# An attention kernel's inner rhythm: products with v in halves of 256 queries, three pairs of scores and three halves in every phase

## The chip, the cores and the metric

The kernel runs on one core of a Trainium2 chip. The metric is the device time of one execution in microseconds. A core has engines that run side by side, each through its own queue in order: TensorE (PE, matmuls; PEld is its loading of weights), VectorE (DVE), ScalarE (ACT), GpSimd (POOL) and SyncE (SP, used here to issue DMAs). They wait for each other by semaphores. TensorE writes its results to PSUM, which has eight banks of 512 float32 columns over 128 partitions.

## The reference, cut to what matters

The input x is (4, 128, 64, 64), float32: four images of 128 channels and 4096 positions. Two layers follow each other. The first is self-attention with 4 heads of 32 channels, on x normalized in 8 groups of channels:

```python
x_norm = _group_norm(x, norm_w, norm_b)
qkv = einsum('oc,bchw->bohw', qkv_w, x_norm) + qkv_b
q, k, v = split(qkv, 3, axis=1)
attn = softmax(einsum('bhid,bhjd->bhij', q, k) * 32 ** -0.5)
out = einsum('bhij,bhjd->bhid', attn, v)
x = x + einsum('oc,bchw->bohw', proj_w, out) + proj_b
```

The second is two 3x3 convolutions with weights quantized to 3 bits, each followed by batch normalization over the whole batch, with relu after the first, and relu of the sum with the layer's input after the second.

## The kernel before, in words

Attention is done in 32 blocks: four images by eight chunks of 512 queries (`blocks`; n is the block's number, b the image, qb the chunk). A block goes through 32 steps of 128 keys (`NK = 32`, kt is the step in the block). A step is:

- two *pairs* of scores (`scores`, line 425), one for heads 0 and 1, one for heads 2 and 3. q and k are held as a high and a low part in a rounded format (float32r), stacked so that two heads use the two halves of 64 rows of the array side by side. A pair is four matmuls of 512 columns, into one PSUM tile s of two banks. Its exponential (line 427, ScalarE, 128 x 1024) writes to the step's tile p in SBUF, which holds all four heads.
- the *products with v* (`weights`, line 438): for each head a float32 product of 128 keys x 32 channels by 512 queries, four heads on four column tiles of the array side by side, accumulated over all 32 steps in one PSUM bank, acc. A float32 product shows in the trace as two matmuls and two weight loads, so a step has eight.
- the addition of p to the running sum of the softmax's denominator (line 450, VectorE, 128 x 2048), or in six steps of a block (`MOVED`) a DMA that adds p to a second sum rm (line 445).

PSUM is full: the pool pss has three tiles s (six banks), psa has two banks, one of which is the block's acc. The other serves all small products, one after another. The pool ppool has eight tiles p; two of them hold the first image's x until its last projection is done, in block 1.

The order on the engines is written by hand (`manual_schedule`). Scores run ahead of products: `run_scores(2)`, and then `for s, w in ((3, 1), (3, 2)): run_scores(s); run_weights(w)`, that is three pairs, one step's products, three pairs, two steps' products, and so on. A run of scores and the run of products after it is called a phase here. Scores and products use the array in different tilings, so each phase changes tiling twice.

Beside this a block has side work, listed by `schedule(n, before)` as (step, function) and called after that step's products:

- for the block before: the sums over keys (l, line 467), their way through DRAM to be inverted and spread (`spread`, `invert`, `gather`), `weigh` (line 514), `project` (po, line 301), and the residual and store;
- for the next image: statistics (gm, gv, gb, lines 249 to 280) and the projections to q, k and v of a chunk of 512 positions (pq, pk, pv, line 301), in two halves each and an evacuation, which for q and k is ScalarE for the high part (line 335) and then VectorE for the low part (line 336), for v VectorE alone (line 355). They are written to DRAM and loaded again as needed. For the first image most of this is in a prelude and in blocks 0 and 1;
- in blocks 25 to 30 the quantization of the convolutions' weights on VectorE (`pieces`).

Small products use the column tiling of the products with v. They are put at `slots`, the steps with (32 n + kt) mod 3 = 0, so at the end of the phases with one step's products. `visit` puts the two halves at one slot or at two, and the evacuation one step later.

After attention come the convolutions (line 722).

Of the kernel before, what the change touches and what calls it, by code (L numbers as in the profile page):

```python
# [25 lines left out]
D = 32  # L26
TAPS = 9
FB = 512
# [50 lines left out]
def _fast_body(ctx, tc, x, norm_w, norm_b, qkv_wt, qkv_b, proj_wt, proj_b,  # L79
               w1, alpha1, gamma1, beta1, w2, alpha2, gamma2, beta2, out, cnt):  # L80
    nc = tc.nc
# [4 lines left out]
    NB = N // FB  # L86
    NK = N // P
    KB = FB // P
# [127 lines left out]
    sums = att.enter_context(tc.tile_pool(name="sums", bufs=2))  # L216
# [5 lines left out]
    def f32(t):  # L222
        return t.bitcast(F32)
# [204 lines left out]

    def weights(step):
        n, kt = divmod(step, NK)
        v = vs[blocks[n][0], kt // KB]
        pt = pts[step]
        if kt == 0:
            acc[n] = psa.tile([P, FB], F32, name=f"acc{n}", tag="a")
        for h in range(HEADS):
            nc.tensor.matmul(acc[n][h * D : (h + 1) * D, :], v[:, kt % KB, h * D : (h + 1) * D],  # L438
                             pt[:, h, :], start=(kt == 0), stop=(kt == NK - 1))
        if kt in MOVED:  # L440
            if kt == MOVED[0]:
                msum[n] = rpool.tile([P, HEADS, FB], F32, name=f"rm{n}", tag="rm")
                nc.gpsimd.dma_start(out=msum[n], in_=pt)  # L443
            else:
                nc.gpsimd.dma_start(out=msum[n], in_=pt, accum_op=ALU.add)  # L445
        elif kt == 1:
            rsum[n] = sums.tile([P, HEADS, FB], F32, name=f"r{n}", tag="r")
            nc.vector.tensor_tensor(rsum[n], pts[step - 1], pt, ALU.add)  # L448
        elif kt > 1:
            nc.vector.tensor_tensor(rsum[n], rsum[n], pt, ALU.add)  # L450
# [123 lines left out]
    def first_chunk(j, what, start):  # L574
        return project_parts(0, j, lambda: halves[j // 4][:, j % 4, :], start)[what]
# [2 lines left out]
        load_k(b, j)  # L578
        load_v(b, j)

    for what, j in (("k", 0), ("q", 0), ("k", 1), ("v", 0), ("k", 2), ("v", 1), ("k", 3), ("v", 2)):
        for f in first_chunk(j, what, True):
            f()
        if what == "v":
            load_k(0, j + 1)


# [1 line left out]
    late, xin = {}, {}  # L589
# [4 lines left out]
    def schedule(n, before):  # L594
        b, qb = blocks[n]
        todo = []
        slots = [kt for kt in range(NK - 1) if (n * NK + kt) % 3 == 0]
        two = b + 1 < B and qb in (2, 3)
        full = two or n == 1

        def add(kt, f):
            todo.append((kt, f))

        def visit(kts, first, second, evacuate=None):
            add(kts[0], first)
            add(kts[-1], second)
            if evacuate:
                add(kts[-1] + 1, evacuate)

        if before:  # L610
            add(1, before["merge"])
            kts = slots[3:4] if full else slots[3:5]
            visit(kts, lambda: before["sums"](0), lambda: before["sums"](1))
            kt = kts[-1]
            add(kt + 1, before["spread"])
            add(kt + 3, before["invert"])
            add(kt + 4, before["gather"])
            add(kt + 6, before["residual"])
            add(slots[9] - 2, before["weigh"])
            add(slots[9], before["project"])  # L620
            add(slots[9] + 1, before["store"])
        if n + 1 < len(blocks):
            add(14, lambda: load_q(*blocks[n + 1]))
        if n == 0:
            for kt, what, j in ((0, "k", 4), (2, "q", 1), (3, "v", 3), (6, "k", 5), (9, "k", 6),
                                (12, "v", 4), (15, "k", 7), (18, "v", 5), (21, "v", 6),
                                (24, "v", 7)):
                visit((kt,), *first_chunk(j, what, False))
                if what == "k":
                    add(kt + 2, lambda j=j: load_k(0, j))  # L630
        if n == 1:
            for i, j in zip((0, 1, 2, 4, 5, 6), range(2, NB)):
                visit(slots[i : i + 1], *first_chunk(j, "q", False))
        if b + 1 < B:
            if qb == 1:
                st = small.tile([P, NB, 6], F32, name=f"st{b + 1}", tag="st")
                for j in range(NB):
                    add(3 * j // 2, lambda j=j: fetch(b + 1, j))
                    add(3 * j // 2 + 3, lambda j=j: nc.vector.bn_stats(st[:, j, :], xin[b + 1, j]))
                late[b] = norm_parts(b + 1, st)  # L640
                add(15, late[b][0])
                for i in (0, 1):
                    add(slots[7 + i], late[b][1 + 2 * i])
                    add(slots[7 + i] + 1, late[b][2 + 2 * i])
            if qb == 2:
                add(slots[0], late[b][5])
                add(slots[0] + 1, late[b][6])
            chunks = {1: (), 2: (0, 1), 3: (2, 3), 4: (4,), 5: (5,), 6: (6,), 7: (7,)}
            for i, j in enumerate(chunks.get(qb, ())):
                p = project_parts(b + 1, j, lambda j=j: xin[b + 1, j])  # L650
                if not two:
                    places = dict(k=slots[0:2], q=slots[5:7], v=slots[7:9])
                elif i == 0:
                    places = dict(k=slots[1:2], q=slots[2:3], v=slots[4:5])
                else:
                    places = dict(k=slots[5:6], q=slots[6:7], v=slots[7:9])
                    add(8, lambda j=j: fetch(b + 1, j))
                for what, kts in places.items():
                    visit(kts, *p[what])
            if qb > 0 and qb + 1 in chunks:  # L660
                add(22, lambda j=chunks[qb + 1][0]: fetch(b + 1, j))
            if qb == NB - 1:
                for j in range(NB - 1):
                    add(4 * j + 1, lambda j=j: load_kv(b + 1, j))
        if b > 0 and qb == 0:
            add(1, lambda: load_kv(b, NB - 1))
        if b == B - 1 and 0 < qb < NB - 1:
            for kt in range(1, NK - 1, 5):
                add(kt, lambda: next(pieces, None))
        if n == len(blocks) - 1:  # L670
            add(5, lambda: load_band(0, 0))
            add(13, lambda: split_band(0, 0))
            add(17, lambda: load_band(0, 1))
            add(24, lambda: split_band(0, 1))
        return sorted(todo, key=lambda t: t[0])

    pieces = (piece for task in quant_tasks(stage) for piece in task())
    steps = len(blocks) * NK
    at = {"pair": 0, "step": 0}
    todo, parts = [], {}  # L680

    def side(kt):
        while todo and todo[0][0] <= kt:
            todo.pop(0)[1]()

    def run_scores(count):
        for _ in range(min(count, 2 * steps - at["pair"])):
            scores(at["pair"])
            at["pair"] += 1

    def run_weights(count):
        for _ in range(min(count, steps - at["step"])):
            n, kt = divmod(at["step"], NK)
            if kt == 0:
                assert not todo
                todo[:] = schedule(n, parts.get(n - 1))
            weights(at["step"])
            at["step"] += 1
            if kt == NK - 2:
                parts[n] = finish_parts(n)  # L700
            if kt == NK - 1:
                parts[n]["copy"]()
            else:
                side(kt)

    run_scores(2)
    while at["step"] < steps:
        for s, w in ((3, 1), (3, 2)):
            run_scores(s)
            run_weights(w)  # L710

# [592 lines left out]
```

## Time and profile before

| | |
|---|---|
| time | 2590.79 us, median of 3 runs (2589.92 to 2592.28) |
| span of the profiled run | 2588.2 us |
| attention, from the first to the last product with v | 34.4 to 2265.8 us |
| PE busy | 2517.2 us (97%) |
| DVE busy | 2140.3 us (83%) |
| ACT busy | 2081.9 us (80%) |
| s, line 425, 8192 matmuls | 1162.3 us busy |
| acc, line 438, 8192 matmuls | 1021.1 us busy |
| chain that ended last | PE 88%, DVE 5%, issue 3%, DMA 2%, ACT 1% |

A row of the profile's groups gives the line of the code, the engine and operation, what it writes and reads with shapes, the count, then busy time and mean duration in ns, and after the second bar the engine's idle time just before these instructions and what ended most of it. "64*128" or "128*32" on a matmul is the part of the array that it uses, rows by columns. The timeline gives start, length, engine, line and a count for a run of equal instructions, with the idle time before it and what ended it in brackets. Matmuls are pipelined: their ends are modelled, and the starts tell more. A row of busy times by stretch gives the stretch, its length and then the busy time (and count) of PE, PEld, DVE, ACT and POOL, the granted clock of TensorE, the share of DMA and GB/s.

### The profile page before, as it was taken

Reading aid. Unit: us, or ns where it says so; the run is one execution under the profiler, and the core shown is the slowest. Engines: PE = TensorE matmul, PEld = TensorE weight load, DVE = VectorE, ACT = ScalarE, POOL = GpSimd, SP = SyncE. Lnnn points to the kernel's source line nnn. Section 1 sums busy time; section 2 is a strip of 40 time slices with the busy share of each in tenths; the row PEclk is TensorE's granted clock in tenths of the full one; section 3 lists DMA queues with packets and bytes.
Section 4 is the critical chain, followed back from the end, with each engine's and each line's share of the span. In section 5 each row is a group of like instructions: output and inputs, shape, how many; then the busy total and the mean of one; then the engine's idle time right before and its main releaser. Section 6 shows DMA issues by size and latency. Waiting matters only on the chain.

```text
span 2588.2 us, 48399 instructions
## 1 busy us (share of the span) xinstructions
PE 2517.2 (97%) x20394; PEld 1223.4 (47%) x20394; DVE 2140.3 (83%) x1402; ACT 2081.9 (80%) x2275; POOL 281.4 (11%) x456
## 2 busy tenths in 40 slices
PE   6999999999999999999999999999999999999894
PEld 3444444444444444444444444444444444477773
DVE  5898888888988898888988988888999998953344
ACT  4888899999988999999988899999889898911223
POOL 2111111111011111110011111110000000100000
PEclk9999999999999999999999999999999999999997
DMA  5876766698667767697667666986655757634004
GB/s 160 191 187 172 177 161 149 154 206 201 162 148 178 178 155 171 149 225 171 160 171 161 164 159 150 207 202 142 151 130 126 154 126 148 146 80 145 1 1 164
DMA packets 147417, 400.04 MB, mean 155 GB/s; under 512 B 59240, under 2 KB 60008, under 8 KB 118648
## 3 DMA queue, kind: packets, MB, share of 16 engines
q0 software_dynamic: 45888, 280.59, 47.9%
q1 hardware_dynamic: 100728, 115.23, 16.8%
q8 instruction: 162, 2.65, 0.4%
q10 hardware_dynamic: 576, 1.05, 0.1%
q14 instruction: 63, 0.52, 0.1%
HBM read 105.32 MB, written 55.83 MB: 62 GB/s over the span
## 4 chain that ended last, share of the span: by engine, by line
PE 88%; DVE 5%; issue 3%; DMA 2%; ACT 1%; POOL 0%; SPq 0%; DVEq 0%; POOLq 0%; ACTq 0%
PE s L425 39%; PE acc L438 34%; PE c L722 9%; DVE r L450 3%; DMA rm<-p 2%; PE l L467 1%; PE po L301 1%; PE pk L301 1%; PE pq L301 1%; PE pv L301 1%; ACT p L427 1%; DVE res L844 1%; DMA xh<-in_x_dram 0%; DMA q<-qst 0%; DVE st L570 0%
## 5 line engine op out<-in xcount | busy, mean ns | idle before, releaser
L427 ACT ACTIVATE p<-s 128x1024 f32<-128x1024 f32 x2048 | 1940.2, 1034 | 235.0 <-PE s L425 158.7
L450 DVE TENSOR_TENSOR r<-r,p 128x2048 f32<-128x2048 f32 x768 | 1758.4, 2290 | 97.3 <-ACT p L427 48.1
L425 PE MATMUL s<-q,k 64*128 64x512 f32 x8192 | 1162.3, 413 | 3.9 <-ACT p L427 2.2
L438 PE MATMUL acc<-p,v 128*32 128x512 f32 x8192 | 1021.1, 601 | 0.6 <-DVE v L355 0.6
L425 PEld LDWEIGHTS s<-q,k 64*128 64x128 f32 x8192 | 711.7, 185 | 631.9 <-issue 298.0
L438 PEld LDWEIGHTS acc<-p,v 128*32 128x32 f32 x8192 | 198.6, 109 | 453.7 <-issue 446.3
L445 POOL DMA_DIRECT2D rm<-p x160 | 138.6, 866 | 950.7 <-ACT p L427 783.6
L775 ACT COPY cv<-c 128x512 f32<-128x512 f32 x64 | 37.6, 587 | 220.8 <-DVE st L774 220.8
L722 PE MATMUL c<-hi,wq 128*128 128x512 f32 x576 | 150.1, 405 | 8.3 <-DVE hi L805 6.8
L722 PE MATMUL c<-lo,wq 128*128 128x512 f32 x576 | 148.1, 402 | 0.0
L774 DVE BATCH_NORM_STATS2 st<-c 128x6 f32<-128x512 f32 x64 | 44.7, 699 | 124.5 <-PE c L722 102.5
L722 PEld LDWEIGHTS c<-hi,wq 128*128 128x128 f32 x576 | 109.4, 191 | 40.1 <-issue 8.9
L722 PEld LDWEIGHTS c<-lo,wq 128*128 128x128 f32 x576 | 109.0, 189 | 28.9
L448 DVE TENSOR_TENSOR r<-p,p 128x2048 f32<-128x2048 f32 x32 | 73.3, 2291 | 25.0 <-ACT p L427 25.0
L336 DVE SCALAR_TENSOR_TENSOR kst<-pk,b,kst 128x512 fp32r<-128x512 f32 x32 | 24.0, 751 | 73.2 <-ACT kst L335 73.2
L336 DVE SCALAR_TENSOR_TENSOR qst<-pq,b,qst 128x512 fp32r<-128x512 f32 x32 | 24.0, 750 | 41.6 <-ACT qst L335 41.6
L471 POOL DMA_DIRECT2D r<-rm x31 | 26.3, 848 | 159.8 <-PE s L425 91.9
L340 POOL DMA_DIRECT2D qd<-qst x31 | 23.3, 753 | 177.6 <-DVE qst L336 130.2
L443 POOL DMA_DIRECT2D rm<-p x32 | 17.8, 556 | 223.3 <-ACT p L427 136.4
L335 ACT ACTIVATE kst<-pk,b 128x512 fp32r<-128x512 f32 x32 | 22.4, 701 | 21.7 <-PE pk L301 21.7
L340 POOL DMA_DIRECT2D kd<-kst x28 | 20.6, 734 | 167.6 <-DVE kst L336 159.6
L467 PE MATMUL l<-r,ones 128*32 128x256 f32 (+1 forms) x504 | 37.9, 383 | 0.5 <-issue 0.5
(129 smaller groups left out, 672.0 us busy)
## 6 DMA issues: line engine op xcount, KB each, us to landing
rm<-p POOLq DMA_DIRECT2D x192, 1024.0 KB, 7.9
q<-qd SPq DMA_DIRECT2D x248, 128.0 KB
r<-rm POOLq DMA_DIRECT2D x31, 1024.0 KB, 7.1
x<-in_x_dram SPq DMA_DIRECT2D x80, 256.0 KB
k<-kd SPq DMA_DIRECT2D x124, 128.0 KB
qd<-qst POOLq DMA_DIRECT2D x31, 512.0 KB, 6.9
kd<-kst POOLq DMA_DIRECT2D x28, 512.0 KB, 4.0
y<-x POOLq DMA_DIRECT2D x32, 256.0 KB, 5.0
```

The lines of the kernel that those rows point to most:

```text
L301: nc.tensor.matmul(out[cs, :], w[:, cs], x, start=True, stop=True)
L336: nc.vector.scalar_tensor_tensor(lo, ps[what], bias, t[:, 0, :], ALU.add, ALU.subtract)
L340: (nc.sync if start else nc.gpsimd).dma_start(out=dst[b, j].rearrange("s p n -> p s n"), in_=t)
L425: nc.tensor.matmul(s[:, i, :], k[r, half, c0 : c0 + P], q[r, half, part, :], start=(part == 0), stop=(part == 1))
L427: nc.scalar.activation(pts[step][:, 2 * half : 2 * half + 2, :], s, AF.Exp, scale=SCALE)
L438: nc.tensor.matmul(acc[n][h * D : (h + 1) * D, :], v[:, kt % KB, h * D : (h + 1) * D], pt[:, h, :], start=(kt == 0), stop=(kt == NK - 1))
L445: nc.gpsimd.dma_start(out=msum[n], in_=pt, accum_op=ALU.add)
L448: nc.vector.tensor_tensor(rsum[n], pts[step - 1], pt, ALU.add)
L450: nc.vector.tensor_tensor(rsum[n], rsum[n], pt, ALU.add)
L467: nc.tensor.matmul(t["l"][h * D : (h + 1) * D, cs], ones, r[:, h, cs], start=first, stop=end)
L722: nc.tensor.matmul(ps[:, j, :].rearrange("p (r w) -> p r w", w=W), w[:, tap, :], part[:, j * RB + kh : j * RB + kh + RB, kw : kw + W], sta ...
L774: nc.vector.bn_stats(st[:, b * NB + c, :], ps[:, j, :])
```

## The change

The products with v of a step are made in two halves of 256 queries, so that the work can be cut at half steps. Every phase is now three pairs of scores and three halves, where it was three pairs and one step or two. `weights(step, half)` computes 256 columns of acc for all heads; the first half of step 0 carries the start flag for the bank, the second half of the last step the stop flag. The sum of the denominators and the moving DMAs stay once in a step, after its second half. Six pairs of scores, where it was five, run ahead of the first product.

The side work is placed by halves: p counts halves in a block (0 to 63), `ends` are the last halves of phases, which is every third, and the products may stand at any of them (where before they stood at the end of every second phase). `visit(i, ...)` puts the halves of a small product at `ends[i]` and `ends[i + 1]`, or both at `ends[i]` with `split=False`, and the evacuation at the half after. The places in blocks 0 and 1 are laid out anew: the projection of v for chunk 3 moves to the prelude, that of q for block 1 from step 2 of block 0 to its step 19, and the load of that q from step 14 to step 24.

```diff
-    def weights(step):
+    def weights(step, half):
...
-        if kt == 0:
+        if kt == 0 and half == 0:
             acc[n] = psa.tile([P, FB], F32, name=f"acc{n}", tag="a")
+        cs = slice(half * FB // 2, (half + 1) * FB // 2)
         for h in range(HEADS):
-            nc.tensor.matmul(acc[n][h * D : (h + 1) * D, :], v[:, kt % KB, h * D : (h + 1) * D],
-                             pt[:, h, :], start=(kt == 0), stop=(kt == NK - 1))
+            nc.tensor.matmul(acc[n][h * D : (h + 1) * D, cs], v[:, kt % KB, h * D : (h + 1) * D],
+                             pt[:, h, cs], start=(kt == 0 and half == 0),
+                             stop=(kt == NK - 1 and half == 1))
+        if half == 0:
+            return
...
-    for what, j in (("k", 0), ("q", 0), ("k", 1), ("v", 0), ("k", 2), ("v", 1), ("k", 3), ("v", 2)):
+    for what, j in (("k", 0), ("q", 0), ("k", 1), ("v", 0), ("k", 2), ("v", 1), ("k", 3), ("v", 2),
+                    ("v", 3)):
...
-        slots = [kt for kt in range(NK - 1) if (n * NK + kt) % 3 == 0]
+        ends = [p for p in range(2 * NK - 2) if (2 * n * NK + p) % 3 == 2]
...
-            kts = slots[3:4] if full else slots[3:5]
-            visit(kts, lambda: before["sums"](0), lambda: before["sums"](1))
...
-            add(slots[9] - 2, before["weigh"])
-            add(slots[9], before["project"])
-            add(slots[9] + 1, before["store"])
+            e = visit(5 if two else 6, lambda: before["sums"](0), lambda: before["sums"](1),
+                      split=not two)
...
+            at_half(ends[18] - 4, before["weigh"])
+            at_half(ends[18], before["project"])
+            at_half(ends[18] + 2, before["store"])
         if n + 1 < len(blocks):
-            add(14, lambda: load_q(*blocks[n + 1]))
+            add(24 if n == 0 else 14, lambda: load_q(*blocks[n + 1]))
         if n == 0:
-            for kt, what, j in ((0, "k", 4), (2, "q", 1), (3, "v", 3), (6, "k", 5), (9, "k", 6),
-                                (12, "v", 4), (15, "k", 7), (18, "v", 5), (21, "v", 6),
-                                (24, "v", 7)):
-                visit((kt,), *first_chunk(j, what, False))
+            for i, what, j in ((0, "k", 4), (2, "k", 5), (4, "v", 4), (6, "k", 6), (8, "v", 5),
+                               (10, "k", 7), (12, "q", 1), (14, "v", 6), (16, "v", 7)):
+                visit(i, *first_chunk(j, what, False), split=False)
...
         if n == 1:
-            for i, j in zip((0, 1, 2, 4, 5, 6), range(2, NB)):
-                visit(slots[i : i + 1], *first_chunk(j, "q", False))
+            for i, j in zip((0, 2, 8, 10, 12, 14), range(2, NB)):
+                visit(i, *first_chunk(j, "q", False), split=False)
...
-                    add(slots[7 + i], late[b][1 + 2 * i])
-                    add(slots[7 + i] + 1, late[b][2 + 2 * i])
+                    at_half(ends[13 + 2 * i] + (n > 1), late[b][1 + 2 * i])
+                    at_half(ends[13 + 2 * i] + 3, late[b][2 + 2 * i])
...
-    run_scores(2)
-    while at["step"] < steps:
-        for s, w in ((3, 1), (3, 2)):
-            run_scores(s)
-            run_weights(w)
+    run_scores(3)
+    while at["half"] < 2 * steps:
+        run_scores(3)
+        run_weights(3)
```

More of the change, by code (lines that the diff above doesn't have):

```diff
@@ L579, in load_kv @@
         load_v(b, j)
-    for what, j in (("k", 0), ("q", 0), ("k", 1), ("v", 0), ("k", 2), ("v", 1), ("k", 3), ("v", 2)):
+    for what, j in (("k", 0), ("q", 0), ("k", 1), ("v", 0), ("k", 2), ("v", 1), ("k", 3), ("v", 2),
+                    ("v", 3)):
         for f in first_chunk(j, what, True):
             f()
-        if what == "v":
+        if what == "v" and j < 3:
             load_k(0, j + 1)
@@ L596, in schedule, with at_half @@
         todo = []
-        slots = [kt for kt in range(NK - 1) if (n * NK + kt) % 3 == 0]
+        ends = [p for p in range(2 * NK - 2) if (2 * n * NK + p) % 3 == 2]
         two = b + 1 < B and qb in (2, 3)
-        full = two or n == 1
+        def at_half(p, f):
+            todo.append((p, f))
         def add(kt, f):
[L602 to L606, printed above, removed]
+            todo.append((2 * kt + 1, f))
@@ L607, in visit @@
+        def visit(i, first, second, evacuate=None, split=True):
+            at_half(ends[i], first)
+            e = ends[i + 1 if split else i]
+            at_half(e, second)
             if evacuate:
-                add(kts[-1] + 1, evacuate)
+                at_half(e + 1, evacuate)
+            return e
         if before:
             add(1, before["merge"])
-            kts = slots[3:4] if full else slots[3:5]
-            visit(kts, lambda: before["sums"](0), lambda: before["sums"](1))
@@ L614, in schedule @@
[L614 to L618, printed above, removed]
-            add(slots[9] - 2, before["weigh"])
-            add(slots[9], before["project"])
-            add(slots[9] + 1, before["store"])
+            e = visit(5 if two else 6, lambda: before["sums"](0), lambda: before["sums"](1),
+                      split=not two)
+            at_half(e + 2, before["spread"])
@@ L622, in schedule @@
+            at_half(e + 6, before["invert"])
+            at_half(e + 8, before["gather"])
+            at_half(e + 12, before["residual"])
+            at_half(ends[18] - 4, before["weigh"])
+            at_half(ends[18], before["project"])
+            at_half(ends[18] + 2, before["store"])
         if n + 1 < len(blocks):
-            add(14, lambda: load_q(*blocks[n + 1]))
+            add(24 if n == 0 else 14, lambda: load_q(*blocks[n + 1]))
         if n == 0:
-            for kt, what, j in ((0, "k", 4), (2, "q", 1), (3, "v", 3), (6, "k", 5), (9, "k", 6),
-                                (12, "v", 4), (15, "k", 7), (18, "v", 5), (21, "v", 6),
-                                (24, "v", 7)):
-                visit((kt,), *first_chunk(j, what, False))
+            for i, what, j in ((0, "k", 4), (2, "k", 5), (4, "v", 4), (6, "k", 6), (8, "v", 5),
+                               (10, "k", 7), (12, "q", 1), (14, "v", 6), (16, "v", 7)):
+                visit(i, *first_chunk(j, what, False), split=False)
@@ L629, in schedule @@
                 if what == "k":
-                    add(kt + 2, lambda j=j: load_k(0, j))
+                    at_half(ends[i] + 5, lambda j=j: load_k(0, j))
         if n == 1:
-            for i, j in zip((0, 1, 2, 4, 5, 6), range(2, NB)):
-                visit(slots[i : i + 1], *first_chunk(j, "q", False))
+            for i, j in zip((0, 2, 8, 10, 12, 14), range(2, NB)):
+                visit(i, *first_chunk(j, "q", False), split=False)
         if b + 1 < B:
@@ L642, in schedule @@
                 for i in (0, 1):
-                    add(slots[7 + i], late[b][1 + 2 * i])
-                    add(slots[7 + i] + 1, late[b][2 + 2 * i])
+                    at_half(ends[13 + 2 * i] + (n > 1), late[b][1 + 2 * i])
+                    at_half(ends[13 + 2 * i] + 3, late[b][2 + 2 * i])
             if qb == 2:
-                add(slots[0], late[b][5])
-                add(slots[0] + 1, late[b][6])
+                at_half(ends[0], late[b][5])
+                at_half(ends[0] + 1, late[b][6])
             chunks = {1: (), 2: (0, 1), 3: (2, 3), 4: (4,), 5: (5,), 6: (6,), 7: (7,)}
@@ L651, in schedule @@
                 if not two:
[L652 to L656, printed above, removed]
+                    for what, i in dict(k=1, q=10, v=13).items():
+                        visit(i, *p[what])
+                    continue
+                for what, i in (dict(k=2, q=7, v=9) if i == 0 else dict(k=11, q=13, v=15)).items():
+                    visit(i, *p[what], split=False)
+                if j in (1, 3):
                     add(8, lambda j=j: fetch(b + 1, j))
-                for what, kts in places.items():
-                    visit(kts, *p[what])
             if qb > 0 and qb + 1 in chunks:
@@ L678, in _fast_body, with side @@
     steps = len(blocks) * NK
-    at = {"pair": 0, "step": 0}
+    at = {"pair": 0, "half": 0}
     todo, parts = [], {}
-    def side(kt):
-        while todo and todo[0][0] <= kt:
+    def side(p):
+        while todo and todo[0][0] <= p:
             todo.pop(0)[1]()
@@ L691, in run_weights @@
     def run_weights(count):
-        for _ in range(min(count, steps - at["step"])):
-            n, kt = divmod(at["step"], NK)
-            if kt == 0:
+        for _ in range(min(count, 2 * steps - at["half"])):
+            n, p = divmod(at["half"], 2 * NK)
+            if p == 0:
                 assert not todo
                 todo[:] = schedule(n, parts.get(n - 1))
-            weights(at["step"])
-            at["step"] += 1
-            if kt == NK - 2:
+            weights(*divmod(at["half"], 2))
+            at["half"] += 1
+            if p == 2 * NK - 3:
                 parts[n] = finish_parts(n)
-            if kt == NK - 1:
+            if p == 2 * NK - 1:
                 parts[n]["copy"]()
             else:
-                side(kt)
-    run_scores(2)
-    while at["step"] < steps:
-        for s, w in ((3, 1), (3, 2)):
-            run_scores(s)
-            run_weights(w)
+                side(p)
+    run_scores(3)
+    while at["half"] < 2 * steps:
+        run_scores(3)
+        run_weights(3)
     bandlist = [(b, g) for b in range(B) for g in range(H // BR)]
```

## The prediction

> **What bounds the kernel now.** I read the page first (busy shares, then the chain), then busy times by stretch, then TensorE's timeline where no side product runs.
>
> ```profile
> PE 2517.2 (97%) x20394; PEld 1223.4 (47%) x20394; DVE 2140.3 (83%) x1402; ACT 2081.9 (80%) x2275; POOL 281.4 (11%) x456
> ...
> L427 ACT ACTIVATE p<-s 128x1024 f32<-128x1024 f32 x2048 | 1940.2, 1034 | 235.0 <-PE s L425 158.7
> L450 DVE TENSOR_TENSOR r<-r,p 128x2048 f32<-128x2048 f32 x768 | 1758.4, 2290 | 97.3 <-ACT p L427 48.1
> L425 PE MATMUL s<-q,k 64*128 64x512 f32 x8192 | 1162.3, 413 | 3.9 <-ACT p L427 2.2
> L438 PE MATMUL acc<-p,v 128*32 128x512 f32 x8192 | 1021.1, 601 | 0.6 <-DVE v L355 0.6
> L438 PEld LDWEIGHTS acc<-p,v 128*32 128x32 f32 x8192 | 198.6, 109 | 453.7 <-issue 446.3
> ```
>
> TensorE is busy 97% and is 88% of the chain. By the groups it hardly ever idles (3.9 and 0.6 us before its two great lines), but ends of matmuls are modelled, so waits under a pipelined matmul's modelled tail don't show as idle. They show in the timeline. This is TensorE alone in block 31:
>
> ```profile
> 2203.93 1.83 PE L425 MATMUL s<-q,k 64*128 64x512 f32 x12
> 2205.69 1.92 PE L438 MATMUL acc<-p,v 128*32 128x512 f32 x16
> 2207.55 1.66 PE L425 MATMUL s<-q,k 64*128 64x512 f32 x12
> 2209.14 1.06 PE L438 MATMUL acc<-p,v 128*32 128x512 f32 x8
> 2210.14 1.83 PE L425 MATMUL s<-q,k 64*128 64x512 f32 x12
> ```
>
> One score phase is always 12 matmuls, three pairs. After two steps of products with v (x16) it takes 1.66 us, after one step (x8) 1.83. The timeline of all engines at such a phase says why: the weight load for the third pair waits for an exponential.
>
> ```profile
> 1206.33 0.76 PEld L425 LDWEIGHTS s<-q,k 64*128 64x128 f32 x8 [0.84 <-ACT p L427]
> 1206.33 1.83 PE L425 MATMUL s<-q,k 64*128 64x512 f32 x12
> 1207.43 0.30 PEld L425 LDWEIGHTS s<-q,k 64*128 64x128 f32 x4 [0.34 <-ACT p L427]
> ```
>
> There are three score banks (pool pss), so pair n+3 needs the exponential of pair n. From raw starts: score matmuls follow each other every 232 ns, but the third pair starts 292 ns after its predecessor and its second half 337 later: 60 ns of waiting and 105 of restart, 0.165 us, the difference of 1.83 and 1.66. A score phase with a side product before it doesn't wait (block 10):
>
> ```profile
> 753.82 1.07 PE L438 MATMUL acc<-p,v 128*32 128x512 f32 x8
> 754.70 1.05 PE L301 MATMUL pk<-x,wn 128*32 128x256 f32 x16
> 755.68 1.67 PE L425 MATMUL s<-q,k 64*128 64x512 f32 x12
> ```
>
> So the waits sit in cycles without side products. Added up from start-to-start gaps over the trace, everything above 232 ns inside score phases is 27.4 us: 16.7 in blocks 0 to 24 and 10.7 in blocks 25 to 31. The page agrees: 8192/12 = 682.7 phases x 1.66 = 1133, against 1162.3 busy, 29 over.
>
> One stretch has another limit. Busy by stretch, blocks 24, then 25 to 28 (weights quantized on VectorE), then the last three:
>
> ```profile
> 1721.40:1788.50 67.10, 67.10 (x538) 28.53 (x540) 59.08 (x31) 60.48 (x66) 6.20 (x8) 1.00 0.70 158
> 1788.50:2066.50 278.00, 273.25 (x2156) 116.37 (x2148) 263.51 (x207) 244.96 (x267) 25.01 (x32) 0.99 0.63 140
> 2066.50:2265.80 199.30, 199.30 (x1586) 84.59 (x1584) 182.80 (x104) 179.44 (x194) 18.99 (x29) 1.00 0.64 138
> ```
>
> The fields are length, then PE, PEld, DVE. VectorE is at 95% in the middle one and PE idles 4.75 us, all before the projection: the list of waits has PE po behind DVE av (the product of line 514), 4.8 us in 3 waits.
>
> **The skill.** "TensorE: Matmul & The Clock Gate", section Back-to-back issue gap, gives columns over clock plus a fixed 2.5 ns per matmul. The trace agrees: groups of four products on four column tiles start every 429 to 430 ns at 512 columns and every 216 at 256 (l, pk, pq), that is 426.7 + 2.7 and 213.3 + 2.7. "TensorEngine Tiling (Array Packing)", Key Properties, says that changing tiling mode drains the engine. The trace agrees: last product to first score is 542 ns where 429 is normal, first score to second 340 where 232 is, and the first product follows 326 after the last score, with 454 to the second: some 0.34 us for each pair of switches. "PSUM — Partial Sum Buffer", The four PSUM rules, says that a first-matmul flag clears a whole bank and that a later one without it overwrites where bits are clear; so half 1 may go without a start, and costs no clearing.
>
> **The change, part by part.**
>
> *Phases of 3 and 3 for 3,1 and 3,2.* Per three steps there are still six pairs, three steps and four switches, so no drain is saved or added. From a score phase's start to the next, without a wait: 2210.14 - 2207.55 = 2.59 us with one step; half a step is 0.43; so 3.02. The exponentials: the first starts 0.78 after the score phase's start, they follow every 0.91, and the third ends 3.64 after it (read at 1203.74: ends at 1207.38). Now the third pair is wanted 1.04 after a phase start: in the short phase at 2.59 + 1.04 = 3.63, too early by what is seen; in an even phase at 3.02 + 1.04 = 4.06, with 0.37 to spare beyond a hop of 0.05. ScalarE needs 3 x 0.91 = 2.74 of 3.02. The waits go: -27.4.
>
> *VectorE's stretch.* In blocks 26 and 28 a faster PE only meets VectorE at the projection, as it does now. I leave them their share (2.1 + 1.5): +3.6.
>
> *Halves.* Each step has four pass groups of 256 for two of 512: 4 x 216.0 - 2 x 429.3 = 5.4 ns, x 1024 = +5.5 us. Twice as many weight loads of 109 ns lie beside passes of 216; pk, l and pq of the same shape run with no gap, and pv of 128 columns at 109 ns, so neither loading nor issue binds. Of a phase's three halves the latest need is the first exponential of the same phase, for the third half: ready 0.78 + 1.03 = 1.8 after the phase start, wanted at 1.27 (last score) + 0.33 + 0.24 + 3 x 0.216 = 2.5. No wait.
>
> *Side products at all ends.* Same matmuls, in the same tiling mode as the products with v, at ends of phases as before: no cost by themselves. A bank of psa still has two phases between most products. Their evacuations on ScalarE (0.70 us for k and q, 0.59 for copies, some 0.1 of it overlapped) stand between exponentials: with one, the third exponential ends 0.3 later than 3.64, just inside 4.06 - 0.05. I allow +2 for those that don't fit (127 such evacuations, a wait of 0.1 to 0.2 in one of eight or so). Queued behind are the exponentials, and PE for them.
>
> *Block 0.* Now q for block 1 follows k4 by two steps and v3 follows q by one, and both wait for VectorE's evacuation of the one free bank (1.52 and 2.38 us in brackets), after which the clock halves for a phase:
>
> ```profile
> 41.29 1.07 PE L301 MATMUL pq<-xh,wn 128*32 128x256 f32 x16 [1.52 <-DVE kst L336]
> ...
> 47.33 1.25 PE L301 MATMUL pv<-wn,xh 128*32 128x128 f32 x32 [2.38 <-DVE qst L336]
> 48.50 2.93 PE L425 MATMUL s<-q,k 64*128 64x512 f32 x12
> ```
>
> With v3 in the prelude (0.87 us of PE, beside the wait for q's first load) and three steps between others these go: -1.5 - 2.4 - (2.93 - 1.66) = -5.2. Starting with six pairs for five delays the first product by one exponential and a restart, less than 1.2: +1.2. The q product of block 1 comes at step 19 with its load at step 24, needed by about step 29. Eight issues at some 0.5 to 0.75 us and a landing of about 5 (q's first copies took 4.7) against 5 steps x 2.1: bound 0 to 3, I take +1.
>
> *Block 1.* The product q7 is put at the end where gm is only then read out; PE may wait behind VectorE's additions (2.29 each): 0 to 3, I take +1. Fetch and load moves otherwise lie beside PE.
>
> Sum: -27.4 + 3.6 + 5.5 + 2 - 5.2 + 1.2 + 1 + 1 = -18.3; 2590.8 - 18.3 = 2572.5 us.
>
> **Rivals.** (a) *ScalarE's waits only move.* Evacuations use up the 0.37 us, and VectorE, at 88% in the steady blocks, meets evacuations half a step earlier and waits for ScalarE (now 73 us over 32 of kst, 2.3 each) with additions queued behind; p tiles then come free late. Half of the 27.4 stays: 2586. For it: ScalarE is 90% busy in block 24. Against: blocks 4 to 7 with these evacuations have only 0.3 to 0.4 us of excess now. (b) *VectorE's stretch gains as well*, because its waits at the projection shrink with the even rhythm, and the allowances (4 us) aren't needed: -18.3 - 3.6 - 4 = 2565. Against: line 450 and the quantization are untouched. (c) *Slower.* New waits of a microsecond per block: scores now run one more pair ahead in every other phase, so a p tile lives 0.5 us longer, while adding DMAs hold it 7.9 us (one of 14 is in the chain at 160); with two of eight tiles holding x in blocks 0 and 1 this bites first. 32 x 1 - 18.3 = +14: 2604. Against: now all exponentials wait for such DMAs only 4.1 us in 5 waits. If each of the 2048 added pass groups exposed its load of 109 ns it would be +223, which the 216 ns of l rules out.
>
> **Numbers.** Forecast 0.6, (a) 0.16, (b) 0.12, (c) 0.12. Range 2560 to 2588: the low end is (b) with the waits at the projection gone too (-4.8), the high end (a) and a little more; (c) is left out. A time under 2585.6 is faster, over 2596 slower: forecast, (b) and over half of (a), which lies at that edge, make 0.81 faster; the rest of (a) and the edge of (c) 0.08 the same; the rest of (c) 0.11 slower.
>
> **What would show it.** Right: score phases of 12 at 1.66 throughout and no 1.83; L425 busy near 1135; products x24 of 256 columns at 216; phase to phase 3.03; no bracketed waits before pq and pv in block 0. Wrong: a score phase over 1.75 in blocks 3 to 24; 256-column groups slower than 220; PE idle before q, l or gm in blocks 0 and 1; VectorE or ScalarE above 95% in steady blocks.

## The result: 2605.7 us for 2590.9, slower by 0.57%

| | before | after |
|---|---|---|
| time, median | 2590.85 us | 2605.72 us |
| ratio, 95% interval | | 1.0057 (1.0039 to 1.0074) |
| span of the profiled run | 2588.2 us | 2604.2 us |

The forecast was 2572.5 us and faster; the time lies above its range and on the other side. It is close to the 2604 of the rival (c); how far (c) was right is said below. These lines of the page of after answer to those shown of before; lines 427 and 425 are as they were, line 450 is now 454, line 438 is now 439.

```profile
PE 2510.7 (96%) x28586; PEld 1491.3 (57%) x28586; DVE 2139.2 (82%) x1402; ACT 2086.3 (80%) x2275; POOL 281.6 (11%) x456
...
PE s L425 35%; PE acc L439 31%; PE c L729 9%; DMA rm<-p 6%; DVE r L454 5%; PE po L301 1%; PE l L471 1%; PE pk L301 1%; PE pq L301 1%; ACT p L427 1%; PE pv L301 1%; DVE res L851 1%; DMA tk<-in_L_conv_w_dram 0%; DMA xh<-in_x_dram 0%; DVE qst L336 0%
...
L427 ACT ACTIVATE p<-s 128x1024 f32<-128x1024 f32 x2048 | 1950.3, 1032 | 245.7 <-PE s L425 181.1
L425 PE MATMUL s<-q,k 64*128 64x512 f32 x8192 | 1146.0, 411 | 15.8 <-ACT p L427 14.5
L439 PE MATMUL acc<-p,v 128*32 128x256 f32 x16384 | 1029.2, 384 | 1.0 <-DVE v L355 1.0
```

PE's busy time fell by 6.5 us while the span grew by 16. The scores are busy for 16 us less and now have 14.5 us of real idle time in front of them, ended by exponentials, and the DMAs that add p to rm make 6% of the chain, where they made 2%. So the short waits went and others came. TensorE's timeline in block 24 has both:

```profile
1738.55 1.50 PE L439 MATMUL acc<-p,v 128*32 128x256 f32 x24
1739.98 1.66 PE L425 MATMUL s<-q,k 64*128 64x512 f32 x12
1741.58 1.50 PE L439 MATMUL acc<-p,v 128*32 128x256 f32 x24
1743.01 1.19 PE L425 MATMUL s<-q,k 64*128 64x512 f32 x8
1745.06 0.73 PE L425 MATMUL s<-q,k 64*128 64x512 f32 x4 [0.85 <-ACT p L427]
```

A phase is x12 at 1.66 us and x24, 3.03 us from score to score: as forecast. Then one score phase breaks in two. The timeline of ScalarE at that place says what it waited for:

```profile
1743.98 3.77 ACT L427 ACTIVATE p<-s 128x1024 f32<-128x1024 f32 x4 [1.29 <-DMA rm<-p]
```

The exponential had no free p tile, since a moving DMA was still reading the oldest one. ScalarE's waits for such DMAs (us in total, times, longest), before and then after:

```profile
ACT p L427 <- DMA rm<-p: 4.1, 5, 2.1
...
ACT p L427 <- DMA rm<-p: 23.6, 17, 2.9
```

The lengths of the stretches (us, cut at the first product with v of a block), with and without the moving DMAs (experiment 2):

| blocks | before | after | before, no moving DMAs | after, no moving DMAs |
|---|---|---|---|---|
| 0 | 79.4 | 72.8 | 79.5 | 72.8 |
| 1 | 76.2 | 81.6 | 74.3 | 82.4 |
| 2 to 24 | 1598.5 | 1615.0 | 1597.7 | 1594.5 |
| 25 to 28 | 278.0 | 279.6 | 274.6 | 273.2 |
| 29 to 31 | 199.3 | 197.4 | 199.6 | 197.1 |

Block 0 gained, block 1 lost, and blocks 2 to 24 lost 16 where they should have gained.

### The profile page after: what moved, and what is told of

The parts are those of the page before. It is cut to its first block, busy times and chain, and to the rows that moved or that the text cites. A ratio compares the mean times of both kernels' runs of the same rounds, so it can differ in the third digit from the quotient of the medians.

```text
span 2604.2 us, 64736 instructions
## 1 busy us (share of the span) xinstructions
PE 2510.7 (96%) x28586; PEld 1491.3 (57%) x28586; DVE 2139.2 (82%) x1402; ACT 2086.3 (80%) x2275; POOL 281.6 (11%) x456
## 4 chain that ended last, share of the span: by engine, by line
PE 80%; DVE 8%; DMA 7%; issue 4%; ACT 1%; POOL 0%; SPq 0%; DVEq 0%; POOLq 0%; ACTq 0%
PE s L425 35%; PE acc L439 31%; PE c L729 9%; DMA rm<-p 6%; DVE r L454 5%; PE po L301 1%; PE l L471 1%; PE pk L301 1%; PE pq L301 1%; ACT p L427 1%; PE pv L301 1%; DVE res L851 1%; DMA tk<-in_L_conv_w_dram 0%; DMA xh<-in_x_dram 0%; DVE qst L336 0%
## 5 line engine op out<-in xcount | busy, mean ns | idle before, releaser
L425 PE MATMUL s<-q,k 64*128 64x512 f32 x8192 | 1146.0, 411 | 15.8 <-ACT p L427 14.5
L439 PE MATMUL acc<-p,v 128*32 128x256 f32 x16384 | 1029.2, 384 | 1.0 <-DVE v L355 1.0
L439 PEld LDWEIGHTS acc<-p,v 128*32 128x32 f32 x16384 | 462.9, 109 | 486.9 <-issue 250.8
L449 POOL DMA_DIRECT2D rm<-p x160 | 139.1, 870 | 866.2 <-ACT p L427 625.4
L301 PE MATMUL po<-av,wp 128*32 128x512 f32 x256 | 35.2, 624 | 9.1 <-DVE av L518 9.1
```

The lines of the kernel that those rows point to most:

```text
L301: nc.tensor.matmul(out[cs, :], w[:, cs], x, start=True, stop=True)
L425: nc.tensor.matmul(s[:, i, :], k[r, half, c0 : c0 + P], q[r, half, part, :], start=(part == 0), stop=(part == 1))
L439: nc.tensor.matmul(acc[n][h * D : (h + 1) * D, cs], v[:, kt % KB, h * D : (h + 1) * D], pt[:, h, cs], start=(kt == 0 and half == 0), stop= ...
```

## The experiments

Each run's ratio is to the kernel before, run beside it on the same chip, and the interval behind it is the 95% one. "After" is the changed kernel. It was timed in four executions (2601.8 to 2609.4 us), and its own interval is 4.5 us to either side, so a gain that is given against it is uncertain by some 5 us.

**1. Halves alone.** In the kernel before:

```diff
-        for h in range(HEADS):
-            nc.tensor.matmul(acc[n][h * D : (h + 1) * D, :], ...
+        for half in range(2):
+            cs = slice(half * FB // 2, (half + 1) * FB // 2)
+            for h in range(HEADS):
+                nc.tensor.matmul(acc[n][h * D : (h + 1) * D, cs], ...
```

> The kernel before, with its own rhythm and places of side work, only each step's products made in two halves of 256 queries one after the other. Theory that halves cost what the pass groups say: 1024 steps x 5.4 ns, +5.5 us, 2596. Rival, that the halves themselves (twice the weight loads) cost what was lost and what was hoped for: +20 us or more, 2611.

2593.9 us, ratio 1.0007 (0.9999 to 1.0016). The busy time of the products is

```profile
L440 PE MATMUL acc<-p,v 128*32 128x256 f32 x16384 | 1026.6, 383 | 0.6 <-DVE v L355 0.6
```

that is 5.5 us over the 1021.1 of before. The halves cost what their pass groups say, or less, and aren't the loss.

**2. No moving DMAs, in both kernels.**

```diff
         if kt in MOVED:
-            if kt == MOVED[0]:
-                msum[n] = rpool.tile(...)
-                nc.gpsimd.dma_start(out=msum[n], in_=pt)
-            else:
-                nc.gpsimd.dma_start(out=msum[n], in_=pt, accum_op=ALU.add)
+            pass
```

> The kernel before without the DMAs that add p to rm, and without the merge: six of 32 steps are left out of the denominators. Every theory: ScalarE waits for these DMAs 4.1 us now, so 2586 to 2590; it is the base for the run beside it.

> The changed kernel without the DMAs that add p to rm, and without the merge: six of 32 steps are left out of the denominators. Theory that p tiles held by late moving DMAs are what the even rhythm ran into: the long waits of score phases in blocks 3 to 24 go, and the time falls by 20 us or more, to 2585 or below; what is left over the forecast are the waits in blocks 1, 2, 10, 26 and 28. Rival, that places of side products and their evacuations cost it: the long waits stay and it is above 2600.

Before: 2583.8 us, ratio 0.9971 (0.9960 to 0.9981), 7 us less, a little more than was expected. After: 2578.0 us, ratio 0.9946 (0.9930 to 0.9963), 28 us less. So the moving DMAs and what they do to other transfers cost the changed kernel some 20 us more than the kernel before, and the changed kernel without them is the faster of the two. Its timeline of TensorE at the same place in the program, block 24:

```profile
1730.02 1.63 PE L425 MATMUL s<-q,k 64*128 64x512 f32 x12
1731.58 1.50 PE L439 MATMUL acc<-p,v 128*32 128x256 f32 x24
1733.01 1.65 PE L425 MATMUL s<-q,k 64*128 64x512 f32 x12
1734.60 1.50 PE L439 MATMUL acc<-p,v 128*32 128x256 f32 x24
```

In each block from 2 to 31 all score phases together exceed their 1.66 us by less than 0.2 us, but for block 28, where one phase takes 2.93 us after its wait for the projection. So evacuations on ScalarE, for which the forecast kept 2 us, don't reach TensorE. These are the scores without moving DMAs, before and then after:

```profile
L425 PE MATMUL s<-q,k 64*128 64x512 f32 x8192 | 1159.6, 412 | 2.0 <-DMA q<-qst 1.6
...
L425 PE MATMUL s<-q,k 64*128 64x512 f32 x8192 | 1141.1, 410 | 2.5 <-DMA q<-qst 1.9
```

But without moving DMAs the change is worth only 5.9 us (2583.8 to 2578.0), a third of the 18.3 that were forecast. By the table block 0 gives 6.7 us, blocks 2 to 24 give 3.2 and blocks 25 to 31 give 3.9, and block 1 takes 8.1 back.

**What makes them late.** Worked out from the instructions and landings in the traces, mean over all blocks, in us: how long after its step's last exponential a moving DMA goes out, and how long after that it lands.

| step | 4 | 9 | 14 | 19 | 24 | 28 |
|---|---|---|---|---|---|---|
| before: goes out | 3.1 | 1.3 | 0.8 | 1.1 | 1.2 | 2.5 |
| before: lands | 5.2 | 7.7 | 8.8 | 9.4 | 8.7 | 7.8 |
| after: goes out | 5.7 | 1.7 | 1.3 | 2.6 | 4.3 | 5.0 |
| after: lands | 5.4 | 7.9 | 8.9 | 11.3 | 8.3 | 8.1 |

A tile's exponential and the one that takes the tile again lie 15.3 to 15.8 us apart before and 15.0 to 16.3 after, by step, so the time to reuse has hardly changed; the DMA takes more of it. At steps 9 and 14 it goes out 0.4 to 0.5 us later, about what one more pair of scores ahead would make; at the other steps 1.5 to 3.1 us later. The timeline of block 7 shows one (GpSimd's queue is POOL):

```profile
584.71 0.75 DVE L336 SCALAR_TENSOR_TENSOR qst<-pq,b,qst 128x512 fp32r<-128x512 f32 x1 [1.94 <-PE s L425]
...
585.76 0.75 POOL L340 DMA_DIRECT2D qd<-qst  x1 [9.46 <-DVE qst L336]
...
586.51 0.90 POOL L449 DMA_DIRECT2D rm<-p  x1
...
600.81 3.77 ACT L427 ACTIVATE p<-s 128x1024 f32<-128x1024 f32 x4 [2.55 <-DMA rm<-p]
601.20 2.94 SPq L394 DMA_DIRECT2D k<-kd  x4
601.23 0.84 POOL L449 DMA_DIRECT2D rm<-p  x1 [7.29 <-DMA rm<-p]
601.89 0.73 PE L425 MATMUL s<-q,k 64*128 64x512 f32 x4 [1.67 <-ACT p L427]
```

The store of q (qd) stands on GpSimd's queue and waits there for VectorE's evacuation. The moving DMA of step 19 stands behind it, goes out 0.75 us after it (3.3 us after its exponential, where it was 0.3 before), runs beside it and beside the loads of k, and lands after 14.2 us, where it was 8.3. The next moving DMA adds to the same rm and has to wait for that landing (7.29 us of idle queue), so it is late as well, and so is the third. Before the change q was evacuated one and a half to four and a half steps later in the block (three in block 7), after step 19's DMA had gone.

That covers the going out, not the longer landing. In the twelve blocks without a chunk to project (8, 9, 16, 17 and 24 to 31) no store stands between step 19's DMA and the moving DMA before it. There it goes out after 0.3 us and still lands after 11.8 us, for 8.8 before the change. So the longer landing doesn't need the store of q. It goes with the gather (rc, on SyncE's queue), which the change also issues earlier in the block. In nine of the twelve blocks the gather now goes out 0.5 to 2.0 us ahead of step 19's DMA, and that lands after 11.9 to 13.5 us; in the other three it goes out behind, and the landing is 9.1 to 10.7. Before the change only block 31 has it ahead, and lands after 12.5, the others after 7.0 to 9.7.

Two later runs test this, though they were not made for it. Experiments 6 and 8 move the sums of the last image, and the gather with them, ahead of step 14's DMA, and the long landing moves along. In joined_six, in seven of the blocks 24 to 31 (all but 27), step 14's DMA lands after 12.1 to 13.4 us, where after has 6.9 to 9.4, and step 19's after 7.0 to 9.6, where after has 9.1 to 13.5. The residual's load moves with the gather; which of the two lengthens the landing is not separated.

**3. q and v later.**

```diff
-                    for what, i in dict(k=1, q=10, v=13).items():
+                    for what, i in dict(k=1, q=12, v=15).items():
```

> The changed kernel with the projection of q at ends 12 and 13 in place of 10 and 11, and of v at 15 and 16 in place of 13 and 14, in the blocks with one chunk (qb 4 to 7). Theory that the store of q, issued just ahead of the moving DMA of step 19, is what makes that DMA land late (11.3 us in the mean, up to 15.4): landing of step 19's falls towards 9, ScalarE's wait for rm from 23.6 us to under 12, the time by 8 to 12 us, to about 2596. Rival, that one pair more of lead is the cause whatever the place: the waits and 2606 stay.

2596.1 us, ratio 1.0018 (1.0011 to 1.0024): 10 us less by this edit, as expected. ScalarE's wait for rm is 13.9 us in 10 places, where under 12 was expected. The landing of step 19's did not fall (11.4 us), against the expectation; what fell is when it goes out, 1.5 us for 2.6, and step 24's, 3.1 for 4.3, and of the eight blocks in which the tile of step 19 was waited for one is left. So the place on the queue is shown (q and v moved together); that q's store lengthens the landing is not. The rival in part stays open: the lead of one more pair was not changed alone in any run.

**4. Five moving DMAs a block in images 0 to 2**, at steps 4, 10, 16, 22, 28, on top of that.

```diff
-        if kt in MOVED:
+        if kt in (MOVED if blocks[n][0] == B - 1 else (4, 10, 16, 22, 28)):
```

> The changed kernel with q and v two ends later as in q_later, and with five moving DMAs a block in place of six, at steps 4, 10, 16, 22, 28, in the first three images. Theory that what is left of the waits for rm in blocks 8, 16 and 24 comes from moving DMAs that queue behind each other (a landing of 8 to 11 us against 10 us between them, 8 at the last): ScalarE's wait for rm from 13.9 us to under 3, the time 7 to 9 us below q_later's 2596, to about 2588. Rival, that VectorE with 27 additions a block in place of 26 becomes the limit: 2596 or more.

2594.1 us, ratio 1.0006 (0.9997 to 1.0015), a quarter of what was expected, and hardly clear of noise. ScalarE's wait for rm fell to 8.0 us, where under 3 was expected. The wait of block 8 went, that of block 24 stayed, and block 1 became 2.4 us longer. It has one more addition on VectorE, whose evacuations its products wait for; that this is the reason was not tested.

**5. Block 1 and gb.** In the changed kernel, the main lines:

```diff
-            for i, j in zip((0, 2, 8, 10, 12, 14), range(2, NB)):
+            for i, j in zip((1, 3, 7, 9, 11, 13), range(2, NB)):
-                    at_half(ends[13 + 2 * i] + (n > 1), late[b][1 + 2 * i])
+                    at_half(ends[(15 if n == 1 else 13) + 2 * i] + (n > 1), late[b][1 + 2 * i])
-                at_half(ends[0], late[b][5])
+                at_half(ends[1], late[b][5])
```

> The changed kernel with block 1 laid out anew (q at ends 1, 3, 7, 9, 11, 13, the sums at end 5, gm and gv at ends 15 and 17, the output projection at 19) and with gb and six at end 1 in place of end 0 and the first k at end 3 in blocks 2, 10, 18. Theory that small products that stand one end apart wait for the one free bank of psa, and at end 0 for the copy of acc: the waits of gm, gv, pq and gb (2.5 + 1.9 + 2.3 + 1.2 + 2.1 us on the list) go, with the halved clock after one of them, 8 to 11 us, to about 2596. Rival, that block 1 is slow because x holds two of the eight p tiles: 2603 or more.

The list of PE's waits of after shows what this is about (us in total, times, longest):

```profile
PE gm L249 <- DVE qst L336: 2.5, 1, 2.5
PE pq L301 <- ACT av L464: 2.3, 1, 2.3
PE gb L278 <- ACT av L464: 2.1, 2, 1.1
PE gv L259 <- DVE qst L336: 1.9, 1, 1.9
...
PE pq L301 <- DVE mean L252: 1.2, 1, 1.2
```

The timeline of block 1 of after shows it too:

```profile
160.08 0.74 DVE L336 SCALAR_TENSOR_TENSOR qst<-pq,b,qst 128x512 fp32r<-128x512 f32 x1
160.74 4.61 DVE L454 TENSOR_TENSOR r<-r,p 128x2048 f32<-128x2048 f32 x2
160.88 0.38 PE L249 MATMUL gm<-mv,gavg 128*128 128x1 f32 x2 [2.52 <-DVE qst L336]
...
165.47 1.07 PE L301 MATMUL pq<-xh,wn 128*32 128x256 f32 x16 [1.18 <-DVE mean L252]
```

Products at neighbouring ends, 3 us apart, share the one free bank of psa: gm waits until q has been evacuated, and the next q until gm has been read, which on VectorE's queue stands behind two additions. 2597.8 us, ratio 1.0021 (1.0013 to 1.0028): 8 us less. Block 1 takes 74.0 us for 81.6, and none of the five waits is left on the list. That x holds two of the p tiles, the rival, is not what made block 1 long.

**6. The last image.** The main lines:

```diff
-            e = visit(5 if two else 6, ...
+            e = visit(5 if two or b == B - 1 else 6, ...
...
-            at_half(ends[18] - 4, before["weigh"])
+            at_half(ends[18] - (12 if b == B - 1 else 4), before["weigh"])
```

> The changed kernel with, in the last image, the sums at end 5 at once (so that the gather is ahead of the loads of q and of the quantized weights in SyncE's queue) and weigh eight halves earlier. Theory that the projection in blocks 26 and 28 waits for VectorE only because weigh stands behind a VectorE instruction that waits for the late load of tk, and behind the quantization: the waits of po (9.1 us) and the two phases at half clock after them go, 8 to 11 us, to about 2596. Rival, that VectorE is the limit of these blocks: the waits move to the exponentials, and 3 us or less are gained, 2603.

Block 26 on SyncE's queue before the change:

```profile
1896.95 0.35 SPq L174 DMA_DIRECT2D tk<-in_L_conv_w_dram  x1
...
1904.89 0.54 SPq L511 DMA_DIRECT2D rc<-rd  x1
```

Block 26 of after, in the timeline of all engines:

```profile
1908.00 0.54 SPq L515 DMA_DIRECT2D rc<-rd  x1
1908.64 6.54 SPq L405 DMA_DIRECT2D q<-qd  x8
...
1916.79 0.47 SPq L174 DMA_DIRECT2D tk<-in_L_conv_w_dram  x1
...
1925.87 0.42 DVE L176 TENSOR_SCALAR tk<-tk,inv 128x384 f32<-128x384 f32 x1 [6.01 <-DMA tk<-in_L_conv_w_dram]
...
1931.59 0.69 DVE L518 TENSOR_TENSOR av<-av,rc 128x512 f32<-128x512 f32 x1
...
1932.33 1.93 PE L301 MATMUL po<-av,wp 128*32 128x512 f32 x8 [5.32 <-DVE av L518]
```

On SyncE's queue the load of weights to quantize (tk) stood ahead of the gather (rc), which waits for its source. Now the gather stands ahead of the load of q, and tk behind both. VectorE waits 6.01 us for tk, behind that stand the additions and weigh, and behind weigh PE's projection. In block 28, whose projection waits 3.75 us, VectorE waits for no load; there weigh stands behind quantization and additions.

2601.1 us, ratio 1.0034 (1.0023 to 1.0045), 4.7 us less, hardly clear of noise, where 8 to 11 were expected. Blocks 25 to 28 take 272.1 us for 279.6. The waits of po are off the list, but blocks 27 and 30 then wait for rm (26.1 us on ScalarE in all, for 23.6): the rival had part of it. The edit moves the sums and weigh together. In block 26 tk is still issued behind q (at 1915.33 us of this run) and VectorE starts on it at 1925.53; weigh now runs ahead of it, at 1921.92. So it was weigh's place that helped there, and not an earlier tk.

**7. All of these together.**

> The changed kernel with all of these: q and v later, five moving DMAs in the first three images, block 1 and gb, and the last image. If the causes are what the runs so far say and they add up: 2606 - 10 - 8 - 9 - 9 = 2570, faster than the kernel before by 0.8%. Rival, that a wait removed returns at the next one: 2580 or more.

2578.2 us, ratio 0.9945 (0.9928 to 0.9961). It is faster than both kernels. It is 27.5 us less than after; the four edits alone gave 10, 2, 8 and 5, so within their noise they add up. The expected 2570 was 8 us too low, mostly because edits 4 and 6 fell short.

**8. The output stored later.** In one block of three (2, 5, 8 and so on) of this version the moving DMA of step 28 stands behind the store of the block's output (y), which waits for VectorE on GpSimd's queue. So the projection was put at end 19, with experiment 3's edit alone (store_later) and in two versions joined with 5 and 6 as well (joined_six; joined_five has five moving DMAs in images 0 to 2, but six in blocks 0 and 1).

```diff
-            at_half(ends[18] - 4, before["weigh"])
-            at_half(ends[18], before["project"])
-            at_half(ends[18] + 2, before["store"])
+            at_half(ends[19] - 4, before["weigh"])
+            at_half(ends[19], before["project"])
+            at_half(ends[19] + 2, before["store"])
```

> q_later with the output projection at end 19 in place of 18 in all blocks, so that the store of the block's output, which waits for VectorE on GpSimd's queue, is issued after the moving DMA of step 28 and not ahead of it. Theory that these DMAs come late because of what stands before them in GpSimd's queue: step 28's goes out 2 to 3 us after its exponential in place of 4.7, the waits of blocks 8, 16 and 24 (8 us) go, 2596 becomes 2588. Rival, that the loads of the next image's k and v make them land late in any case: 2594 or more, with the waits in blocks 8 and 24 as they are.

> All changes of places together (q and v later, output projection at end 19, block 1 and gb, the last image), with six moving DMAs in every block. If the queue theory holds: 2578 of all_four less the 3 to 4 us of block 1 under five DMAs and the waits of blocks 24, 27 and 30 (9 us), 2566 to 2570. Rival, waits that return elsewhere: 2576 or more.

> As joined_six, with five moving DMAs in images 0 to 2 from block 2 on. If the moving DMAs are no longer late, six or five make no difference: within 2 us of joined_six. Rival, that they still queue behind each other: 3 us or more faster than joined_six.

In this order: 2607.0 us, ratio 1.0047 (1.0031 to 1.0062); 2594.8, ratio 1.0008 (0.9999 to 1.0016); 2593.8, ratio 1.0006 (0.9998 to 1.0014). The first two missed; the third held, 1.0 us from joined_six. The queue part came in part: in store_later step 28's DMA goes out after 3.6 us for 4.7 (2 to 3 was expected), ScalarE's wait for rm falls to 6.2 us, and blocks 16 and 24 are free of it; block 8 keeps 2.5 us. (It waits for step 28 of block 7, where no store of y stood ahead.) But another wait took its place:

```profile
PE po L301 <- DVE av L518: 22.1, 15, 7.0
```

In twelve blocks of images 0 to 2 PE waits 1.0 us each: weigh, which in q_later came straight behind the evacuation of v, now stands on VectorE's queue behind that evacuation and two or three additions, and VectorE works through these without a gap. The other 10.1 us are in blocks 26 to 28, where q_later has 8.9.

**9. weigh earlier.** joined_six with

```diff
-            pe = ends[19]
-            at_half(pe - (12 if b == B - 1 else 4), before["weigh"])
+            pe = ends[16 if b == B - 1 else 19]
+            at_half(pe - 12, before["weigh"])
```

> joined_six with weigh twelve halves ahead of the projection in all blocks (it was four in images 0 to 2), and the projection of the last image at end 16. Theory that weigh at end 19 less four stood on VectorE's queue behind the evacuation of v, so that the projection waited (po 11.9 us in 12 waits, and 8.2 at the block's end behind the residual): both go, and the waits for rm stay as low as with the store later; 2594.8 - 11.9 - 8.2 - the half clocks after them (2) = 2572, 2566 to 2576, faster than all_four. Rival, that a wait comes back once more at another place: 2580 or more.

2578.8 us, ratio 0.9949 (0.9936 to 0.9963), 16 us less than joined_six. weigh isn't on the list of PE's waits any more; of what attention waits for, apart from the first statistics, these are the longest:

```profile
PE s L425 <- ACT p L427: 8.0, 14, 2.7
...
PE l L471 <- DMA r<-rm: 2.2, 2, 2.1
```

It ends level with all_four, with six moving DMAs in every block, and misses its range of 2566 to 2576 by 3 us: the waits for rm are 12.5 us on ScalarE, in blocks 8 and 28 above all (3.6 and 2.5).

## Why the prediction was wrong

- *The waits of the short phases, -27.4: right in kind, too large.* They are gone, and a phase is 3.03 us as worked out. ScalarE and VectorE keep up. But without moving DMAs the scores' busy time falls by 18.5 us, from 1159.6 to 1141.1. The 27.4 were everything above the normal pitch inside score phases, and some 5 of them lie in five phases of over 2 us, which are slow for other reasons (half clock, or a wait for rm). One of these is block 0's phase at half clock (2.93 - 1.66), which the term of block 0 takes off a second time.
- *Halves, +5.5: right as busy time (+5.5), 2 us in the time* with an interval from 0 to 4. The formula that the working cites is for one matmul. The trace's 429 and 216 ns are for a group of four and fit it only with the columns counted twice, which the working doesn't say; the term rests on the measured starts.
- *Block 0, -5.2 and +1.2: right, with the double count above.* It is 6.6 us shorter and begins 1.5 us later, of which 0.8 us are a longer wait for the first statistics (14.4 us for 13.6).
- *"Side products at all ends: no cost by themselves", +2: this step failed.* It asked whether evacuations delay exponentials on ScalarE. They don't. It did not ask what else moves with the places: the stores to DRAM after an evacuation, which are on GpSimd's queue with the moving DMAs, and the gather behind the sums, beside which these land late. In the place of +2 the runs show some 20 us that come with the moving DMAs: leaving them out saves 28 us after the change and 7 to 8 before it. Of these 20, moving q and v alone gave back 10 (experiment 3); how the rest divides is not shown. The working weighed a late DMA only in rival (c). Its half microsecond of longer life is there at steps 9 and 14, but the lateness at steps 19, 24 and 28 and the queue behind it are not in (c), and 16 of the 17 waits are not in blocks 0 and 1. That its 2604 comes near the measured time is luck.
- *Block 1, +1: mis-sized.* Products one end apart share one bank. The block grew by 5.4 us, and it is as long without the moving DMAs (82.4). Laid out anew, together with gb in blocks 2, 10 and 18, it gave 8 (experiment 5).
- *VectorE's stretch, +3.6 ("as it does now"): mis-sized.* Blocks 25 to 28 went from 278.0 to 279.6, where the forecast has 278.0 - 6.6 + 3.6 + 0.7 = 275.7. The projection's waits grew from 4.8 to 9.1 us: in block 26 an order on SyncE's queue was turned round, so that tk came late with weigh behind it, and in block 28 weigh stood behind quantization and additions. The edit for it gave 4.7 (experiment 6).

The three terms, 20 - 2, 8 - 1 and 279.6 - 275.7, make 29 of the 33 us between 2572.5 and 2605.7, but some 3 us are in them twice: leaving out the moving DMAs shortens blocks 25 to 28 by 6.4 us after the change and by 3.4 before it. The other 7 us aren't assigned, though 27.4 for 18.5 could cover them, and the first two terms are uncertain by some 5 us. Still open: how much of the time the longer landing beside the gather costs; what the one more pair of lead costs by itself; and why blocks 8 and 24 keep their waits in most versions; both follow the block in which the next image's k and v are loaded. A ninth p tile wasn't tried.

## What to carry to other kernels

A regular rhythm on the bounding engine can be worth what its timeline says and still lose, if making it regular moves what hangs on it: for each step that changes its place, list what it issues, on which queue, what that queue holds behind it, and whose buffer the last of those releases. A chain of accumulating DMAs has little slack: here one lands after 8.4 us in the median, and the next goes out some 10.5 us behind it, so one late landing makes the next ones late, and the kernel pays at the buffer, far from the cause. And the waits that went when one product was moved (experiment 8) came back larger at another queue, until the instruction that feeds that product moved too.

## What the runs showed of the hardware that was not expected

After some of its waits TensorE runs at half speed for a while. In block 26 of after the groups of po follow the wait of 5.3 us at 852 ns for 429, and the scores behind them at 427 for 232; the granted clock is 0.50 from 1932.0 to 1938.5 us. Against their usual times this cost 2.1 us beyond the wait. The Trainium skill, "TensorE: Matmul & The Clock Gate", Part 1, puts the limit at an idle window of about 3.4 us that runs freely. Here a wait of 2.3 us (pq at 112.03 in block 1 of after) was followed by the slow pitch as well, with a granted clock of 0.50 from 112.6 to 115.8 us and some 1.5 us lost, while one of 2.5 us in the same block (gm at 160.88) was not: the scores behind it follow each other every 232 ns.

A moving DMA of 1 MB that adds lands after anything from 6.9 to 15.4 us in after (median 8.4). The thirteen that go out within 2.6 us behind a gather land after 11.9 to 13.6 us; the median of the rest is 8.3. The first of a block, a plain copy of the same size, lands after 4.4 to 7.6 us.
